# A transformer block in float32 on one core: the second half's gate and up projections as seven products

## The chip, the cores and the metric

The kernel runs on one core of a Trainium2 chip. The metric is the device time of one execution in microseconds (us); of several runs the median is compared. The core has five engines that run side by side, each through its own queue in order: TensorE (PE, matrix products and transposes; its weight loads are listed as PEld), VectorE (DVE), ScalarE (ACT), GpSimd (POOL) and SyncE (SP), whose queue issues the DMA transfers.

## The reference

The input `x` is 2048 rows of 1024 float32. The block is

```
x = x + layernorm(attention(layernorm(x)))        # 16 heads of 64, causal, rotary
x = x + layernorm(ffn(layernorm(x)))
ffn(y): gate = y @ Wg.T;  up = y @ Wu.T           # Wg, Wu: 2752 x 1024
        inter = silu(gate) * up                   # 2048 x 2752
        return inter @ Wd.T                       # Wd: 1024 x 2752
```

`Wg`, `Wu` and `Wd` come as codes from 0 to 15 (int32) with one scale for each block of 64 inputs. A weight is the code's entry in a fixed table of 16 values times the scale.

## The kernel before

The work has four stages: queries, keys, values and attention; the output projection with its layer norms; gate and up; down. All matrices are float32. Gate/up and down take three matmuls for each product (`mm3`, L110): every operand is split into a rounded high part (`A.copy`, on ScalarE, L120) and the rest (a subtraction on VectorE, L121), and high times high, high times rest and rest times high are summed in one PSUM bank of 128 x 512.

**Projection.** For each row tile `t` of 128 rows, `project` multiplies by `Wo`, whose parts lie in the SBUF slots `w`, `xc` and `pa`. `finish_rows` adds the residual, normalizes and stores the normalized rows to DRAM (`yd`). `fill_x2` reads them back and transposes them on TensorE (8 transposes of 128 x 128 for a row tile), and each transposed piece is split into `x2[c]`, the operand of gate/up for the row block `c` of 512 rows. There are four row blocks; all four are held in SBUF.

**Gate and up.** The 2752 outputs are cut into 22 index tiles of 128 (the last is of 64), taken in the order `PAIRS`: 0, 11, 1, 12 and so on. For one index tile `gate_up_weights` looks up 2048 columns of weights (128 gate and 128 up outputs for each of 8 slices of the inputs), 512 at a time, in `looked_up` (L517): codes and scales are loaded, VectorE converts the codes to float (L530), ScalarE makes five straight or bent lines of the code (L535, L537), VectorE combines them by minimum and maximum and multiplies by the scale (L541 to L545), and `split` makes the two parts in `wt`. Then `gate_up` (L599) runs each of the four row blocks against it: 8 slices x 3 matmuls for gate, the same for up, each into a bank of its own (`any_bank` goes round all eight). ScalarE applies Silu to gate out of its bank (L619), VectorE multiplies by up out of the other (L620).

**What down needs.** Down is done already as seven products of half matrices in place of eight (Strassen's method in Winograd's form, `PRODUCTS`). Its left operands A11, A12, A22, S1 to S4 are combined from the results of gate/up on GpSimd (L632 to L640) and stored in DRAM (`aq`). Its right operands come from `down_weights` (L645), two lookups of 512 columns after each index tile; GpSimd combines them (L665 to L674) and they are stored (`bq`). So of each index tile there are four row blocks of matmuls, four lookups for gate/up and two for down.

The order on each engine is set by a scheduler that takes, by priority in the order of the program, what is ready by its own estimate of time; slots of one tag are handed out as they come free. All the transfers in question are issued from SP's queue, in order.

Of the kernel before, what the change touches and what calls it, by code (L numbers as in the profile page):

```python
# [57 lines left out]
def block_kernel(ctx, tc, x, wq, wk, wv, wo, gu_codes, gu_scales, d_codes, d_scales, cos_sin, out):  # L58
# [11 lines left out]
    SLOTS = {"hd": (7, 8), "w": (3, 8), "xc": (4, 8), "pa": (6, 8), "pb": (2, 4), "f4": (4, 4), "pw": (3, 4), "t2": (3, 2), "ol": (1, 2)}  # L70
# [39 lines left out]
    def mm3(o, w, xx, first, last):  # L110

        r = T.matmul(o, lhsT=w[:, 0], rhs=xx[:, 0], start=first, stop=False)  # L112
        T.matmul(o, lhsT=w[:, 0], rhs=xx[:, 1], start=False, stop=False)  # L113
        T.matmul(o, lhsT=w[:, 1], rhs=xx[:, 0], start=False, stop=last)  # L114
        return r
# [53 lines left out]
    at = [dram.tile([E, 512], F32, tag=f"at{c}", name=f"at{c}") for c in range(NC)]  # L169
    x1d = dram.tile([S, E], F32, tag="x1d", name="x1d")  # L170
# [327 lines left out]
    def finish_rows(t, y, beside=False):  # L498
        residual(t, y, slot("f4" if beside else "pb", [P, E], F32, "x1"))
        load(yd[t], y)  # L500
# [16 lines left out]
    def looked_up(codes, s0, s1, rows, tags=None, m=None):  # L517

        if tags:
            c8, sc = (slot(tag, [P, 512], F32, "cs") for tag in tags)  # L520
        else:
            cs = slot("pw", [P, 2, 512], F32, "cs")
            c8, sc = cs[:, 0], cs[:, 1]
# [4 lines left out]
        if m is None:  # L528
            m = slot("f4", [P, 2, 512], F32, "m")[:, 0]
        V.tensor_scalar(c8, c8.bitcast(I32), 1.0, -8.0, ALU.mult, ALU.add)  # L530

        def line(ab):
            ln = slot("t2", [P, 512], F32, "ln")
# [12 lines left out]
        return m  # L546

    def gate_up_weights(n, tags=None):
        it = PAIRS[n]
        w = it_cols(it)  # L550
        wt = [slot(tag, [P, 2, 4, w], FR, "wt") for tag in ("hd", "pa" if n % 2 else "hd")]
        kk = 512 // w

        def columns_of(k0):
            n = kk * w
            off = it * KE * 256 + k0 * w
            t = wt[k0 // 4][:, :, k0 % 4 : k0 % 4 + kk, :]
            m = looked_up(
                gu_codes[:, off : off + n], gu_scales[0:1, off : off + n], gu_scales[1:2, off : off + n], P, tags
            )  # L560
            split(t[:, 0].rearrange("p k n -> p (k n)"), t[:, 1].rearrange("p k n -> p (k n)"), m)
# [116 lines left out]
    for c in range(2):  # L678
        gate_up(*todo[0], c)
# [163 lines left out]
```

## Time and profile before

| | |
|---|---|
| three runs | 3007.55, 3008.38, 3016.82 us; median 3008.38 |
| span of the profiled execution (first to last instruction) | 3001.2 us; its own time outside the span isn't given |
| granted TensorE clock, mean | 0.995 |
| busy over the span: PE, DVE, ACT, POOL | 2908.5, 2032.8, 1701.8, 953.9 us |
| gate/up matmuls (L112 to L114, `bk<-x,wt`) | 3 x 1376, from 1620.9 to 2570.8 us |
| down matmuls (`bk<-bt,at`) | 3 x 616 |
| gate/up from 1725 to 2475 us: PE, DVE, ACT, POOL busy | 750.0, 519.9, 420.0, 160.5 of 750 us |
| 128 x 512 operations: lookup line on ACT, combination on DVE, on POOL | 717 ns; 685 ns or more; 1290 to 1740 ns |
| 128 x 1024 split: ACT, DVE | 1051 and 1279 ns |
| DMA traffic, mean | 179 GB/s |

How it is read: "busy" is the time in which at least one instruction of the engine is open. Instructions of one engine can overlap, so what one of them takes from the engine is the distance from its start to the next start, where the engine waits for nothing, and not its duration. In a group, `out<-in` are the program's tile names, with partitions x elements.

### The profile page before, as it was taken

To read this page: it belongs to the slowest core of one execution; us is meant where nothing else is said; L and a number is where in the kernel's file an instruction comes from. 1 tells how busy PE (TensorE), PEld (TensorE's weight loads), DVE (VectorE), ACT (ScalarE), POOL (GpSimd) and SP (SyncE) were. 2 spreads that over 40 slices of the span, in tenths; PEclk is the share of its full clock that TensorE was granted. 3 is DMA by queue.
4 is the path that set the end of the run, shared out by engine and by line. 5 is a ranking of instruction groups with operands and counts; after the bars stand their busy time and mean duration, and the time that the engine had idled before them with its cause. 6 is when DMAs were issued, how large, how long until landed. Compare 5 with 4: busy or idle time off the path is not lost.

```text
span 3001.2 us, 42583 instructions
## 1 busy us (share of the span) xinstructions
PE 2908.5 (97%) x14192; PEld 2403.6 (80%) x14192; DVE 2032.8 (68%) x4167; ACT 1701.8 (57%) x3573; POOL 953.9 (32%) x1055
## 2 busy tenths in 40 slices
PE   7989999999998999999999999999999999999998
PEld 6868888787877787777788788888888888888887
DVE  5557778787867777777665766776666678444347
ACT  5256767676766666676555655665555566333234
POOL 4344444443444343454322121222211223100034
PEclk9999999999999999999999999999999999999999
DMA  8787665757557558472456444444434444744446
GB/s 290 276 243 232 219 226 170 231 156 234 165 197 195 170 179 254 139 229 92 123 174 219 129 140 135 153 135 137 139 119 136 136 151 153 254 143 143 150 144 235
DMA packets 271740, 536.01 MB, mean 179 GB/s; under 512 B 22944, under 2 KB 113056, under 8 KB 255648
## 3 DMA queue, kind: packets, MB, share of 16 engines
q1 hardware_dynamic: 269344, 529.10, 54.8%
q10 hardware_dynamic: 2176, 4.19, 0.4%
q8 instruction: 112, 1.84, 0.3%
q14 instruction: 108, 0.88, 0.1%
HBM read 371.98 MB, written 161.22 MB: 178 GB/s over the span
## 4 chain that ended last, share of the span: by engine, by line
PE 77%; DMA 10%; DVE 6%; ACT 4%; issue 2%; POOL 1%; SPq 0%; POOLq 0%; ACTq 0%; DVEq 0%
PE bk L112 14%; PE bk L113 14%; PE bk L114 14%; PE pt L323 6%; PE qkv L112 5%; PE qkv L113 5%; PE qkv L114 5%; PE o L328 3%; PE o L327 3%; PE s L281 3%; PE s L283 3%; DMA wf<-in_wq 1%; DMA xc<-xd 1%; DMA q<-qs 1%; DMA vs<-vo 1%
## 5 line engine op out<-in xcount | busy, mean ns | idle before, releaser
L313 POOL TENSOR_SCALAR prob<-prob,rc 128x512 f32<-128x512 f32 (+3 forms) x640 | 404.0, 652 | 439.8 <-DVE rc L308 239.0
L113 PE MATMUL bk<-x,wt 128*128 128x512 f32 x1376 | 535.2, 389 | 0.0
L114 PE MATMUL bk<-x,wt 128*128 128x512 f32 x1376 | 535.0, 389 | 0.0
L112 PE MATMUL bk<-x,wt 128*128 128x512 f32 x1376 | 533.8, 390 | 1.0 <-ACT x L120 0.5
L291 ACT ACTIVATE prob<-s,mxs 128x512 f32<-128x512 f32 (+3 forms) x640 | 402.0, 631 | 148.4 <-DVE mxs L289 90.8
L121 DVE TENSOR_TENSOR pw<-pt,pw 128x512 fp32r<-128x512 f32 (+3 forms) x640 | 378.7, 602 | 120.6 <-ACT pw L120 118.7
L537 ACT ACTIVATE ln<-cs,bias 128x512 f32<-128x512 f32 x520 | 360.0, 717 | 112.4 <-DVE m L544 28.6
L120 ACT CAST pw<-pt 128x512 fp32r<-128x512 f32 (+3 forms) x640 | 323.6, 526 | 168.8 <-PE pt L323 137.8
L323 PE MATMUL pt<-ident,prob 128*128 128x128 f32 x2176 | 344.1, 274 | 7.3 <-DVE pw L121 6.1
L323 PEld LDWEIGHTS pt<-ident,prob 128*128 128x128 f32 x2176 | 266.3, 141 | 62.1 <-issue 7.2
L112 PEld LDWEIGHTS bk<-x,wt 128*128 128x128 f32 x1376 | 258.3, 188 | 55.3 <-ACT wt L120 1.2
L114 PEld LDWEIGHTS bk<-x,wt 128*128 128x128 f32 x1376 | 258.3, 188 | 53.9
L113 PEld LDWEIGHTS bk<-x,wt 128*128 128x128 f32 x1376 | 258.4, 188 | 53.2
L289 DVE TENSOR_REDUCE mxs<-s 128x1 f32<-128x512 f32 x384 | 261.2, 682 | 58.2 <-PE s L283 57.1
L281 PE MATMUL s<-k,q 128*128 128x512 f32 (+3 forms) x640 | 264.0, 414 | 22.9 <-ACT prob L291 18.9
L328 PE MATMUL o<-pw,v 128*128 128x512 f32 (+3 forms) x640 | 246.5, 387 | 9.5 <-DVE pw L121 8.7
L327 PE MATMUL o<-pw,v 128*128 128x512 f32 (+3 forms) x640 | 243.1, 380 | 9.6 <-ACT pw L120 7.2
L112 PE MATMUL qkv<-xc,w 128*128 128x512 f32 x576 | 230.2, 400 | 10.5 <-DMA xc<-xd 5.0
L113 PE MATMUL bk<-bt,at 128*128 128x512 f32 x616 | 239.6, 389 | 0.0
L114 PE MATMUL bk<-bt,at 128*128 128x512 f32 x616 | 238.8, 389 | 0.0
L112 PE MATMUL bk<-bt,at 128*128 128x512 f32 x616 | 238.7, 389 | 0.0
L283 PE MATMUL s<-k,q 128*128 128x512 f32 (+3 forms) x640 | 234.7, 369 | 0.0
(150 smaller groups left out, 5518.2 us busy)
## 6 DMA issues: line engine op xcount, KB each, us to landing
xc<-xd SPq DMA_DIRECT2D x96, 1024.0 KB, 9.2
q<-qs SPq DMA_DIRECT2D x128, 256.0 KB, 7.2
ast<-S SPq DMA_DIRECT2D x44, 512.0 KB, 3.8
cs<-in_gu_scales SPq DMA_DIRECT2D x172, 128.0 KB, 3.3
cs<-in_gu_codes SPq DMA_DIRECT2D x86, 256.0 KB, 3.0
A<-in SPq DMA_DIRECT2D x66, 256.0 KB, 2.1
S<-in SPq DMA_DIRECT2D x66, 256.0 KB, 3.1
ast<-A SPq DMA_DIRECT2D x33, 512.0 KB, 4.4
```

The costliest lines, as they stand in the source:

```text
L112: r = T.matmul(o, lhsT=w[:, 0], rhs=xx[:, 0], start=first, stop=False)
L113: T.matmul(o, lhsT=w[:, 0], rhs=xx[:, 1], start=False, stop=False)
L114: T.matmul(o, lhsT=w[:, 1], rhs=xx[:, 0], start=False, stop=last)
L121: return V.tensor_tensor(lo, src, f32(hi), ALU.subtract)
L281: mm = T.matmul(s, lhsT=q[:, 0, j * P : (j + 1) * P], rhs=k[:, b:e], start=True, stop=False)
L283: T.matmul(s, lhsT=q[:, 1, j * P : (j + 1) * P], rhs=k[:, b:e], start=False, stop=True)
L291: A.activation(prob[i][:, j, : e - b], s, AF.Exp, bias=mx, scale=sign, accum_out=sums[:, j % BATCH, i : i + 1])
L313: G.tensor_scalar(p, p, rc[:, jj % BATCH, i : i + 1], 0.0, ALU.mult, ALU.add)
L323: T.transpose(pt[:, j * P : (j + 1) * P], prob[kb // 4][:, j, kb % 4 * P : (kb % 4 + 1) * P], ident)
L327: T.matmul(o[:, cs], lhsT=v[:, kb, :], rhs=pw[:, 0, cs], start=kb == 0, stop=False)
L328: T.matmul(o[:, cs], lhsT=v[:, kb, :], rhs=pw[:, 1, cs], start=False, stop=kb == nk - 1)
L537: A.activation(ln, c8, AF.Prelu, bias=bias_of[ab], scale=ab[0], alpha=ab[2])
```

## The change

Row blocks 0 and 1 (the first 1024 rows) are worked on as before, for all 22 index tiles, in a first pass. Meanwhile the looked-up weights are combined on GpSimd into seven right operands for each index tile (`keep_weights`) and stored in DRAM (`wqd`). Row blocks 2 and 3 follow in a second pass: rows x inputs and inputs x (gate, up) are each cut in 2 x 2 blocks, and seven products of 4 slices x 3 matmuls take the place of eight (class `Group`). Its left operands (A11, A12, A22 and the sums S1 to S4 of the normalized rows) are combined on GpSimd in `finish_rows`, stored in `yq`, read back and transposed by `fill`; its right operands are read back from `wqd` and split anew (`fetch_w`). Four partial sums share a bank and are copied out between additions. Gate times up for these rows moves from VectorE to GpSimd. The last, half-wide index tile is multiplied out as before.

Lookups for gate and up become 1024 wide; the conversion of codes moves from VectorE to GpSimd. The lookups for down move to the second pass, with slots of their own (`tmp`; 14 KB that a smaller DMA scratch, `dynamic_dma_scratch_size`, sets free). On the host the columns of codes and scales are put in another order.

```diff
     def finish_rows(t, y, beside=False):
...
+        i, l, r = t % 4, y[:, :512], y[:, 512:]
+        if t < 8:
+            load(yd[t], y)
+        elif t < 12:
+            load(yq["A11"][:, i], l)
+            load(yq["A12"][:, i], r)
+        else:
+            load(yq["A22"][:, i], r)
+            a = slot("f4", [P, 2, 512], F32, "ya")
+            for j, name in enumerate(("A11", "A12")):
+                load(a[:, j], yq[name][:, i])
+            s1, s2, s3, s4 = (slot("tmp", [P, 512], F32, "ys") for _ in range(4))
+            G.tensor_tensor(s1, l, r, ALU.add)
...
-        V.tensor_scalar(c8, c8.bitcast(I32), 1.0, -8.0, ALU.mult, ALU.add)
+        G.tensor_scalar(c8, c8.bitcast(I32), 1.0, -8.0, ALU.mult, ALU.add)
...
+    def keep_weights(n, m):
...
+            t1, t2, t3, t4 = (slot("tmp", [P, 512], F32, "wd") for _ in range(4))
+            (b11, b12), (b21, b22) = [[m[:, h, a] for a in range(2)] for h in range(2)]
+            G.tensor_tensor(t1, b12, b11, ALU.subtract)
+            G.tensor_tensor(t3, b22, b12, ALU.subtract)
+            G.tensor_tensor(t2, b22, t1, ALU.subtract)
+            G.tensor_tensor(t4, b21, t2, ALU.subtract)
+            kept = (b11, b21, t2, t1, t3, t4, b22)
+        for i, part in enumerate(kept):
+            load(wqd[n][:, i], part)
+    def gate_up_weights(n):
+        it, wt, w = room_w(n)
+        c = 4 * w
+        m = slot("xc", [P, 2, 2, 512] if w == 256 else [P, 2, 512], F32, "m")
+        for h in range(2):
+            cs = slot("w", [P, 2, c], F32, "cs")
...
+            looked_up(*of_columns(it * KE * 256 + h * c, c), P, mh, cs[:, 0], cs[:, 1], "pw")
...
+            split(*(wt[h][:, i].rearrange(flat) for i in range(2)), mh)
+        keep_weights(n, m)
+        return it, wt, w
...
+    def fill(name, tags, of=any_bank):
+        rows = [slot("pw", [P, 2, 512], F32, "yr") for _ in range(2)]
+        for i in range(2):
+            load(rows[i], yq[name][:, 2 * i : 2 * i + 2])
+        xo[name] = [slot(tag, [P, 2, 2, 512], FR, "x2") for tag in tags]
+        for k in range(4):
+            pt = of()
+            for t in range(4):
+                T.transpose(pt[:, t * P : (t + 1) * P], rows[t // 2][:, t % 2, k * P : (k + 1) * P], ident)
+            d = xo[name][k // 2]
+            split(d[:, 0, k % 2], d[:, 1, k % 2], pt)
+    def fetch_w(n):
+        parts = []
+        for i in (0, 2) if n == NIT - 1 else (0, 2, 4, 6):
+            j = min(2, (3 if n == NIT - 1 else 7) - i)
+            st = slot("pw", [P, 2, 512], F32, "ws")[:, :j]
+            load(st, wqd[n][:, i : i + j])
...
+            split(t[:, 0, :j], t[:, 1, :j], st)
...
     for n in range(NIT):
+        if n == 0:
+            todo.append(gate_up_weights(1))
+        if n == NIT - 1:
+            fill("A12", ("xc", "xc"))
+            fill("S2", ("w", "w"))
+            fill("S1", ("w", "pa"))
+        for c in range(2):
+            gate_up(*todo[n], c)
+        if 0 < n < NIT - 1:
+            todo.append(gate_up_weights(n + 1))
+        if n == NIT - 2:
+            fill("A11", ("xc", "xc"))
...
+    def times(o, name, w, start):
+        for k in range(4):
+            mm3(o, w[:, :, k * P : (k + 1) * P], xo[name][k // 2][:, :, k % 2], start and k == 0, k == 3, True)
+    class Group:
...
+        def one(self):
+            self.y = any_bank()
+            self.inter = room_of(self.kt, self.later, 1)
+            times(self.y, "A11", self.w["B11"], True)
+            A.copy(self.inter[:, 0], self.y)
+        def two(self):
+            x = any_bank()
+            times(x, "A12", self.w["B21"], True)
+            V.tensor_tensor(self.inter[:, 0], self.inter[:, 0], x, ALU.add)
+            A.activation(self.inter[:, 0], self.inter[:, 0], AF.Silu)
+        def six(self):
+            times(self.y, "S2", self.w["T2"], False)
+            self.u2 = slot("tmp", [P, 512], F32, "u2")
+            A.copy(self.u2, self.y)
+        def five(self):
+            self.z = any_bank()
+            times(self.z, "S1", self.w["T1"], True)
+        def seven(self):
+            times(self.y, "S3", self.w["T3"], False)
+            A.copy(self.inter[:, 1], self.y)
+            V.tensor_tensor(self.inter[:, 1], self.inter[:, 1], self.z, ALU.add)
+        def four(self):
+            times(self.y, "A22", self.w["T4"], False)
+            g = slot("tmp", [P, 512], F32, "g2")
+            A.activation(g, self.y, AF.Silu)
+            G.tensor_tensor(self.inter[:, 1], self.inter[:, 1], g, ALU.mult)
+        def three(self):
+            times(self.z, "S4", self.w["B22"], False)
+            V.tensor_tensor(self.u2, self.u2, self.z, ALU.add)
+            G.tensor_tensor(self.inter[:, 0], self.inter[:, 0], self.u2, ALU.mult)
+            for odd in range(2):
+                made(self.kt, self.later, 1, odd)
...
+    for n in range(NIT - 1):
+        now.one()
+        if before:
+            before.four()
+        else:
+            fill("S3", ("hd", "hd"), of_t)
+        now.two()
+        if before:
+            before.three()
+        else:
+            fill("A22", ("hd", "hd"), of_t)
+        ahead = Group(n + 1) if n < NIT - 2 else fetch_w(NIT - 1)
+        now.six()
+        if not before:
+            fill("S4", ("pa", "pa"), of_t)
+        now.five()
+        now.seven()
+        for j in range(2):
+            down_weights(n // 2, 2 * (n % 2) + j)
+        now, before = ahead, now
...
+    last_tile(2, (("A11", now[0]), ("A12", now[1])))
+    before.four()
+    for kt in range(2):
+        ready["A11", kt] = fetch("A11", "B11", kt, True)
+    last_tile(3, (("S1", now[0]), ("A22", now[2])))
+    before.three()
```

`made` holds the combinations and stores that stood at the end of `gate_up` (L632 to L640).

## The prediction

> **What bounds the kernel now.** I read the engine shares on the page first, then the busy time by stretch for the gate/up stage, then TensorE's instructions in order of time, then VectorE and GpSimd side by side.
>
> ```profile
> span 3001.2 us, 42583 instructions
> PE 2908.5 (97%) x14192; PEld 2403.6 (80%) x14192; DVE 2032.8 (68%) x4167; ACT 1701.8 (57%) x3573; POOL 953.9 (32%) x1055
> ```
>
> TensorE is the busiest engine, but an average over stages does not say what the stage to be changed can bear. In the steady part of gate/up:
>
> ```profile
> core 0: us, PE busy (x) PEld busy (x) DVE busy (x) ACT busy (x) POOL busy (x), PEclk, DMA share, GB/s
> 1725.00:2475.00 750.00, 750.00 (x3311) 621.23 (x3310) 519.92 (x762) 420.01 (x656) 160.50 (x104) 1.00 0.42 138
> ```
>
> TensorE never pauses, at the full granted clock (1.00). VectorE is at 69%, ScalarE at 56%. What a matmul costs must not be read from its duration:
>
> ```profile
> 1900.16 0.39 PE L112 MATMUL bk<-x,wt 128*128 128x512 f32 x1
> 1900.39 0.39 PE L113 MATMUL bk<-x,wt 128*128 128x512 f32 x1
> 1900.62 0.39 PE L114 MATMUL bk<-x,wt 128*128 128x512 f32 x1
> ```
>
> One lasts 0.39 us, but the next starts 0.23 us later: they overlap. 750 us / 3311 = 0.2265 us is the price of one. One index tile (192 matmuls) takes 43.5 us of TensorE. The last view is two engines at the same moment, VectorE above and GpSimd below:
>
> ```profile
> 1809.94 0.68 DVE L541 SCALAR_TENSOR_TENSOR mb<-ln 128x512 f32<-128x512 f32 x1
> 1810.54 1.79 DVE L545 TENSOR_TENSOR m<-m,cs 128x512 f32<-128x512 f32 x1
> 1812.25 1.77 DVE L542 SCALAR_TENSOR_TENSOR mb<-ln,mb 128x512 f32<-128x512 f32 x1
> 1814.13 1.60 DVE L543 TENSOR_TENSOR mb<-mb,ln 128x512 f32<-128x512 f32 x1
> 1815.65 0.68 DVE L121 TENSOR_TENSOR wt<-m,wt 128x512 fp32r<-128x512 f32 x1
> ```
>
> ```profile
> 1810.10 1.67 POOL L636 TENSOR_TENSOR in<-in 128x512 f32<-128x512 f32 x1 [17.72 <-DVE in L620]
> 1811.85 1.62 POOL L638 TENSOR_TENSOR in<-in 128x512 f32<-128x512 f32 x1
> 1813.55 1.62 POOL L640 TENSOR_TENSOR in<-in 128x512 f32<-128x512 f32 x1
> ```
>
> While GpSimd combines tiles, VectorE's operations on two SBUF tiles stretch from 0.68 to 1.6 to 1.8 us. Undisturbed they start 0.605 us apart; here three take 1815.65 - 1810.54 = 5.11 us instead of 1.81, so one GpSimd operation takes 1.1 us from VectorE. Operations with one input in PSUM (L620) stayed between 682 and 692 ns in the whole stretch.
>
> **Matmuls removed.** Per index tile the last 1024 rows now need 7 products of 4 x 3 = 12 matmuls, 84, instead of 96. The half-width last tile keeps 48. 21 x 12 = 252 x 0.2265 = 57.1 us less, all on the path, as TensorE never pauses there.
>
> **Transposes added.** Rows 8 to 15 took 8 x 8 = 64, seven operand matrices take 7 x 16 = 112. Eight of them fill 1584.28 to 1585.08 before the next matmul starts, 0.10 us each: 48 x 0.10 = 4.8 us more. TensorE: -52.3 us.
>
> **The first 1024 rows.** Weights for one tile must now come within 96 x 0.2265 = 21.7 us, half of before. VectorE per tile: two halves of five lookup operations and one split, 1024 wide; two 1024-wide splits in the down stage start 1.14 us apart (2643.67, 2644.81), so 12 x 1.14 = 13.7 us. Two multiplications by `u`: 1.2 us. GpSimd: four subtractions for the kept weights and two for the down operands, plus two code conversions 1024 wide (taken from VectorE). No row has such a conversion on GpSimd; L313, one input, lasts 394 ns at 128 columns and 722 at 512, so about 1.0 to 1.2 us at 1024. If VectorE loses 1.1 us to each of the six and 1.0 to each conversion, it needs 13.7 + 1.2 + 6.6 + 2.0 = 23.5 us, more than TensorE. If it loses what it lost on average in the stretch above (by-form groups of L541 to L545 against 685 ns: 64 us over 104 GpSimd operations, 0.61 each), 13.7 + 1.2 + 8 x 0.61 = 19.8 us and TensorE stays the bound. VectorE will be nearly always busy, which is nearer the first row; but GpSimd can slip in beside the two multiplications and in handovers. I take 22.3 us: 20 tiles x 0.6 = +12 us (0 to +36). ScalarE, by its 1242 ns (1024 wide) rows, 10 x 1.24 + 2 x 1.05 + 2 x 0.59 = 15.7 us, fits.
>
> The rule that speaks against this change is in the Trainium skill, "SBUF — State Buffer", section "Who interferes with whom": a VectorE instruction with two SBUF inputs contends with a GpSimd instruction that reads SBUF, and the later one blocks fully. The rows above agree. Taken strictly it would put the sum at its 23.5 us end, where the trace's average put 19.8; I stand between them.
>
> **The last 1024 rows.** TensorE: 84 x 0.2265 = 19.0 us per tile. VectorE: two down lookups 10 x 0.605 = 6.1, splits of the kept weights 3 x 1.14 + 0.6 = 4.0, three additions 1.8: 11.9 us. GpSimd: two multiplications, two combinations of inter, two of down weights (six), and two conversions 512 wide (seven L313 run in 4.17 us, 0.6 each). VectorE with losses: 11.9 + 8 x 0.61 = 16.8 to 11.9 + 6.6 + 1.2 = 19.7 us. ScalarE: 7.2 lines + 3.7 splits + 3 copies and 2 Silu at 0.6 = 13.9 us. TensorE remains just the bound, but one thing is tight. Matrix 7 accumulates into the bank that product 6 left, and must wait until ScalarE has copied it (`u2`); only product 5 lies between, 2.7 us. Likewise matrix 4 waits for `inter[:, 1]`'s copy with one product between. A copy takes 0.6 us and queues behind lookup lines, which wait for VectorE to free `ln`; the longest such waits near here are 0.9 to 1.4 us. Usually it fits. I take 0.5 us per tile: +10 us (0 to +40).
>
> **Moved and hidden.** The kept weights add 7 stores of 256 KB per tile on SP's queue, behind which the next code loads stand. Stores issue in 0.32 us and wait for GpSimd; three staging slots hold the next loads ahead. If that cover went, one landing (3.0 us) per tile would come on top. Traffic per tile: 4.6 MB in 21.7 us, then 4.5 in 19.0: 212 and 237 GB/s, against 256 carried at 2550 to 2625 with TensorE 75.00 of 75. I cost it at nothing. The down lookups leave the first half for the second with their loads and stores, no more in number. The code conversion now queues on GpSimd behind those subtractions, and ScalarE's lines and VectorE wait for it; with the next codes landed ahead it is early, uncovered it costs about 1 us per half tile.
>
> **Start and hand-over.** `Wo` holds `w` and `xc` until the last projection, so tile 1's lookups (load 3 us, conversion, 23 us with the last rows' normalizing between) end some 30 us after it, while tile 0 covers 22: +8 us (0 to +15). The idle 4.0 us in 1640 to 1725 (81.05 of 85) came from waiting for rows 8 to 15, no longer needed there: -4. Between the halves `fill` needs two of three `pw` slots per matrix and a landing of 4 us: +4 (0 to +10).
>
> **Sum.** -52.3 + 12 + 10 + 8 - 4 + 4 = -22 us. The profiled execution has a span of 3001.2 us; its own time is not given, and the median 3008.4 of the runs is 7.2 above the span, time outside it that I leave as it is. 3008.4 - 22 = 2986.
>
> **Rivals.** *TensorE stays the bound throughout* (VectorE loses 0.61 per GpSimd operation, copies always fit): -52.3 + 4 + 4 = 2964. For it: ScalarE and VectorE average 56 and 69% now, and weights are buffered a tile ahead. Against: VectorE's load rises from 519.9 / 17.24 = 30 of 43.5 us per tile to 22.3 + some 18 of 40.7.
>
> *VectorE and GpSimd serialise fully*: 20 x 1.8 + 21 x 0.7 = 51 on -52.3, plus 8: about 3015, no change. For it: the three rows at 1810. Against: GpSimd is idle in most of VectorE's handovers.
>
> *Slower: the copy out of the shared bank.* If VectorE's lag reaches ScalarE's queue in front of `u2` and the `inter[:, 1]` copy, TensorE pauses twice per tile, 42 places. At 1 us each, the size of the ScalarE waits seen, this is 42 us on the forecast: 3028. It decides from (22 + 9) / 42 = 0.75 us per place. For it: before, eight banks rotate and nothing is accumulated onto after a copy. Against: 2.7 us of cover.
>
> **Chances.** TensorE bound 0.25, forecast 0.36 (its own range 2972 to 2999), no change 0.13, slower 0.26. (0.3%, 9 us, is about what a measurement of this kernel can tell from no change.) Faster is 0.25 + 0.36 = 0.61. The range, 2955 to 3032, reaches from the first rival's lower edge to just past the copy's price.
>
> **What would show it.** Right: 3876 gate/up matmuls still 0.2265 us apart; VectorE over 90% in the first half with 1024-wide operations of 1.2 or 2.2 us; TensorE pauses there put to weights (`wt`). Wrong: TensorE at 100% in both halves (first rival), or matmuls waiting for a ScalarE copy of a bank (slower rival), or for a DMA, which I cost at nothing.

## The result and the profile after

The changed kernel takes 3126.13 us (median of four runs, 3124.70 to 3133.40); the kernel before, run beside it, 3012.55. The ratio is 1.0387, 95% interval 1.0363 to 1.041. It is slower by 114 us, where the forecast was 22 us faster and the range ended at 3032. The whole of TensorE's saving arrived, and more than three times as much was lost in pauses and in the slow matmuls after them.

The page of the changed kernel, for the two lines shown of before:

```profile
span 3124.4 us, 42477 instructions
PE 2906.6 (93%) x13988; PEld 2382.7 (76%) x13988; DVE 2198.3 (70%) x3900; ACT 1759.6 (56%) x3478; POOL 1342.3 (43%) x1288
```

TensorE's share falls from 97% to 93%. Its busy time is the same as before with 204 fewer instructions, which already says that some of them ran slower. GpSimd's work grows from 954 to 1342 us. The span is cut at TensorE's first matmul of each part (`wt` for the first 1024 rows, `wr` for the last, `bt` for down), and this table carries the rest of the text:

| | gate/up begins | second pass | down begins | first pass | second pass | down to the end |
|---|---|---|---|---|---|---|
| before | 1620.9 | | 2571.0 | 950.1 together | | 430.2 |
| after | 1630.0 | 2210.1 | 2687.2 | 580.1 | 477.1 | 437.2 |

Of 123.2 us of span, 9.1 lie ahead of gate/up, 107.1 in its two passes and 7.0 in down. (The span lies 11 us below the median of 3012.55 before and 2 us below that of after; hence 123 here and 114 in the medians. Where a run's own time and span are both listed, as 3126.20 and 3124.4, only 1.8 us lie outside the span, so the profiled execution of before was one of its faster ones.) What TensorE needs is 2064 x 0.2265 + 6.4 for 64 transposes = 474 us in the first pass and 1812 x 0.2265 + 4.8 = 415 in the second. So the passes are 106 and 62 us over need. All these are single executions: in the runs below, a pass that an edit doesn't touch took 577.4 to 586.5 us (first) and 474.7 to 477.6 (second), so differences of that size say nothing.

The busy time by stretch, one row for each part, where before had one row with TensorE at 750.00 of 750:

```profile
core 0: us, PE busy (x) PEld busy (x) DVE busy (x) ACT busy (x) POOL busy (x), PEclk, DMA share, GB/s
1630.00:2210.00 580.00, 504.30 (x2131) 409.23 (x2130) 471.18 (x335) 313.28 (x327) 350.53 (x188) 0.93 0.60 199
2210.00:2687.00 477.00, 434.21 (x1862) 348.71 (x1860) 342.16 (x375) 273.42 (x417) 232.12 (x170) 0.98 0.66 218
2687.00:3115.00 428.00, 421.55 (x1848) 347.72 (x1848) 211.95 (x257) 149.43 (x173) 71.57 (x55) 1.00 0.54 181
```

No engine is busy all the time in either pass, and in both the granted clock is under 1.00. TensorE's waits, 1625 to 2209 above the dots and 2210.5 to 2686 below (engine, waiting line, releaser: sum, times, longest):

```profile
PE bk L112 <- ACT wt L120: 41.9, 6, 20.4
PE bk L114 <- DVE wt L121: 29.3, 13, 6.5
...
PE bk L112 <- ACT in L832: 22.5, 15, 3.5
PE bk L112 <- ACT in L813: 15.3, 8, 3.4
```

The passes wait for different things: the first for the two parts of the weights (`split`), the second for ScalarE's copies out of the shared bank. With the `yr` loads and trifles the waits are 76 and 43 us. The other 30 and 19 us are visible only if TensorE is read in order of time:

```profile
1858.45 0.80 PE L112 MATMUL bk<-x,wt 128*128 128x512 f32 x1 [7.00 <-ACT wt L120]
1859.05 0.63 PE L113 MATMUL bk<-x,wt 128*128 128x512 f32 x1
1866.13 0.80 PE L114 MATMUL bk<-x,wt 128*128 128x512 f32 x1 [6.46 <-DVE wt L121]
1866.73 0.63 PE L112 MATMUL bk<-x,wt 128*128 128x512 f32 x1
1867.15 0.63 PE L113 MATMUL bk<-x,wt 128*128 128x512 f32 x1
...
1869.71 0.44 PE L113 MATMUL bk<-x,wt 128*128 128x512 f32 x1
1869.99 0.40 PE L114 MATMUL bk<-x,wt 128*128 128x512 f32 x1
1870.22 0.39 PE L112 MATMUL bk<-x,wt 128*128 128x512 f32 x1
```

After pauses of 7.00 and 6.46 us the matmuls start 0.60, then 0.43 us apart, not 0.23, until 1869.7. The eight from 1866.13 on took 3.6 us instead of 1.8, on top of the pause. Added up over all starts, such slow matmuls cost 23 us in the first pass and 14 in the second. The rest of the 30 and 19 us (7 and 5) lies at the restarts, some 0.2 us each, since a wait is counted from the end of a matmul and the next would have started before it, and in slow transposes. The Trainium skill, "TensorE: Matmul & The Clock Gate", Part 1, says that the clock is halved after an idle window of about 3.4 us and returns after about as long a busy one; this stretch agrees (3.6 us from 1866.13 to 1869.71). Other places show no such sharp bound: after 2.73 us of pause, at 1706.27, seven matmuls were slow, and after 3.32 us, at 2547.16, they were 0.23 us apart from the second on.

VectorE just ahead of the second of these waits, and GpSimd beside it:

```profile
1857.36 2.10 DVE L559 SCALAR_TENSOR_TENSOR m<-ln,m 128x1024 f32<-128x1024 f32 x1
1859.39 2.29 DVE L121 TENSOR_TENSOR wt<-m,wt 128x1024 fp32r<-128x1024 f32 x1
1861.60 2.05 DVE L560 TENSOR_TENSOR m<-m,cs 128x1024 f32<-128x1024 f32 x1
1863.57 0.68 DVE L680 TENSOR_TENSOR in<-bk,in 128x512 f32<-128x512 f32 x1
1864.17 1.90 DVE L121 TENSOR_TENSOR wt<-m,wt 128x1024 fp32r<-128x1024 f32 x1
```

```profile
1856.13 2.25 POOL L594 TENSOR_TENSOR wd<-m,wd 128x512 f32<-128x512 f32 x1
1858.46 2.13 POOL L595 TENSOR_TENSOR wd<-m,wd 128x512 f32<-128x512 f32 x1
1860.67 1.91 POOL L545 TENSOR_SCALAR cs<-cs 128x1024 f32<-128x1024 int32 x1
1863.73 1.26 POOL L592 TENSOR_TENSOR wd<-m 128x512 f32<-128x512 f32 x1 [1.16 <-DVE m L560]
```

VectorE is without a gap, and beside GpSimd its wide operations last 1.9 to 2.3 us instead of the 1.21 of others in the same pass. TensorE starts 0.06 us after the split of 1864.17 ends. Ahead of that split VectorE worked on lookups (L559, L560) of a later tile.

### The profile page after: what moved, and what is told of

Read it like the earlier page. It is cut to its first block, busy times and chain, and to the rows that moved or that the text cites. A ratio compares the mean times of both kernels' runs of the same rounds, so it can differ in the third digit from the quotient of the medians.

```text
span 3124.4 us, 42477 instructions
## 1 busy us (share of the span) xinstructions
PE 2906.6 (93%) x13988; PEld 2382.7 (76%) x13988; DVE 2198.3 (70%) x3900; ACT 1759.6 (56%) x3478; POOL 1342.3 (43%) x1288
## 5 line engine op out<-in xcount | busy, mean ns | idle before, releaser
L121 DVE TENSOR_TENSOR pw<-pt,pw 128x512 fp32r<-128x512 f32 (+3 forms) x640 | 378.8, 602 | 118.8 <-ACT pw L120 117.0
L552 ACT ACTIVATE ln<-cs,bias 128x512 f32<-128x512 f32 (+1 forms) x360 | 319.7, 908 | 247.7 <-POOL cs L545 128.6
L112 PE MATMUL bk<-x,wt 128*128 128x512 f32 x688 | 277.6, 403 | 41.9 <-ACT wt L120 41.9
L114 PE MATMUL bk<-x,wt 128*128 128x512 f32 x688 | 275.6, 402 | 29.4 <-DVE wt L121 29.3
L112 PE MATMUL bk<-x,wr 128*128 128x512 f32 x604 | 240.4, 401 | 39.8 <-ACT in L832 22.5
L113 PE MATMUL bk<-x,wt 128*128 128x512 f32 x688 | 275.3, 400 | 0.0
L113 PE MATMUL bk<-x,wr 128*128 128x512 f32 x604 | 239.3, 396 | 0.0
L114 PE MATMUL bk<-x,wr 128*128 128x512 f32 x604 | 233.2, 395 | 0.9 <-DVE wr L121 0.8
```

The costliest lines, as they stand in the source:

```text
L121: return V.tensor_tensor(lo, src, f32(hi), ALU.subtract)
L552: A.activation(ln, c8, AF.Prelu, bias=bias_of[ab], scale=ab[0], alpha=ab[2])
```

## The experiments: the first pass

**The order of lookups and splits.** Between 1690 and 2090 the groups of the changed kernel, kept apart by shape, show how many halves (1024 columns, half of a tile's weights) VectorE looked up (first combination) and how many it split:

```profile
L556 DVE SCALAR_TENSOR_TENSOR m<-ln 128x1024 f32<-128x1024 f32 x37 | 65.1, 1761 | 0.4
L121 DVE TENSOR_TENSOR wt<-m,wt 128x1024 fp32r<-128x1024 f32 x32 | 61.6, 1926 | 5.7 <-ACT wt L120 5.7
```

37 against 32: lookups run ahead of the splits, from at most 2 halves at the start of the pass to 6 or 7 at 1950 to 2090. The first experiment holds a lookup's first combination behind the split two halves back.

```diff
-        V.scalar_tensor_tensor(m, line(CODES_9_12), CODES_9_12[3], low, ALU.add, ALU.max)
+        ins = V.scalar_tensor_tensor(m, line(CODES_9_12), CODES_9_12[3], low, ALU.add, ALU.max)
+        if behind:                      # splits[-2]
+            after(ins, behind)
```

> One edit to the changed kernel: on VectorE a half tile's lookup may not start before the split of the half tile two before it (before the edit the order let lookups run up to seven halves ahead of the splits). Theory A, order: the first pass lost some 106 us to what TensorE needs for it because VectorE did lookups that could wait, 5 halves of 11 us each, before splits that TensorE waited for; it gets shorter by about 55 us (35 to 75), to 3070. Theory B, rate: VectorE and GpSimd together need 22 to 23.5 us per tile and set the pace whatever the order; 3126, within 10 us.

Measured: 3075.41 us, ratio 1.0204 (1.0144 to 1.0264); the first pass takes 533.8 us, 46 less, the second pass the same 477. Its waits in the first pass, then its stretch of 400 us, and that of the changed kernel:

```profile
PE bk L112 <- ACT wt L120: 21.7, 2, 19.7
PE bk L114 <- DVE wt L121: 14.4, 8, 4.1
```

```profile
1690.00:2090.00 400.00, 385.48 (x1661) 315.68 (x1660) 380.01 (x247) 248.53 (x246) 279.87 (x140) 0.98 0.66 214
```

```profile
1690.00:2090.00 400.00, 350.92 (x1452) 282.67 (x1451) 387.42 (x246) 248.71 (x244) 277.66 (x140) 0.94 0.65 213
```

VectorE does the same number of operations (247 and 246), but 1661 matmuls fit beside them and not 1452. In this run VectorE made 36 splits in the 400 us: 22.2 us for a tile, with VectorE busy for 21.1 of them, where the prediction had 22.3. The amount of VectorE's work was priced nearly rightly; which of it came first was not looked at.

**GpSimd's subtractions for the kept weights.** They are left out with the order as changed, and then with the lookups held back as well:

```diff
-            G.tensor_tensor(t1, b12, b11, ALU.subtract)   # and t3, t2, t4
-            kept = (b11, b21, t2, t1, t3, t4, b22)
+            kept = (b11, b21, b12, b12, b22, b22, b22)
```

> The changed kernel without the four subtractions per tile of the kept weights on GpSimd; as many tiles are stored, with other contents (this leaves out part of the computation). Theory B, rate: VectorE loses 4 x 1.1 us per tile less, 22 becomes 17.6 us, below TensorE's 21.7, and nearly all of the first pass's pauses and slow clock go: about -90 us, 3036. Theory A, order: the lookups still run ahead of the splits, so no more than half of that goes, -20 to -45 us, 3080 to 3106.

> The lookups held two halves ahead of the splits, as in the run with the split first, and the four subtractions of the kept gate and up weights on GpSimd left out (unsubtracted tiles are kept in their place). The two edits alone took 46 and 61 us off the first pass of 580 us, whose matmuls and transposes need 474. Theory 'two parts of one debt' (VectorE is full, and both the order and GpSimd's subtractions matter only while it is behind): together they take 75 to 85 us, the first pass becomes 495 to 505, and what is left is the pause of about 20 us at the start with the clock after it; the whole about 3045. Rival 'two separate costs': 107 us together, so the first pass reaches its 474, the whole about 3018. If the first pass stays at 519 or more, the order costs nothing once GpSimd is quiet.

Measured: 3057.76 us (ratio 1.0145, 1.0085 to 1.0206) and 3056.45 (1.0142, 1.0099 to 1.0186); first passes of 519.2 and 506.8 us. The costs are not separate (46 and 61 alone, 73 together). Without the subtractions VectorE is seldom behind, and the order matters little (12 us, from 519.2 to 506.8). In the run with both edits, 400 us of the first pass are as full as before the change:

```profile
1690.00:2090.00 400.00, 400.00 (x1767) 331.20 (x1766) 351.16 (x275) 266.17 (x271) 130.99 (x77) 1.00 0.72 232
```

Of the 33 us left over 474, 24 lie ahead of 1690: one wait of 20.7 us for the first parts of tile 1, and slow matmuls after it. The other 9 lie in the `fill`s at the end of the pass, 4.7 of them in waits for `yr` loads.

**That pause at the start.** In the changed kernel it ends at 1672.46, since the first wide lookup operation of VectorE starts only at 1659.90. The load of tile 0's looked-up weights (`wb`, 1 MB, landing after 10.1 us) was issued in this stretch, where the DMA share was 0.99 (1625 to 1650). It was moved to a later tile with the subtractions and stores that use it, on top of the held-back lookups.

```diff
-    load(m, wb); keep_weights(0, m)          # ahead of the first pass
+        if n == 1:                           # inside it
+            load(m, wb); keep_weights(0, m)
```

> The kernel with the splits ahead of later lookups, and in it the reading back and combining of the first tile's kept weights (1 MB read, 7 stores, 4 subtractions) moved from the start of the first pass to behind its second tile. Start theory: the pause of 20 us in front of the second tile comes from transfers and GpSimd work of that moment (the transfers' share was 0.99 there); it falls to 8 us or less and the first pass from 534 to about 515, 3075 to 3057. Rival: the pause is set by the last rows' normalizing in front of the lookups; the pause stays at 18 us or more, 3075 within 8.

Measured: 3079.04 us (1.0228, 1.0178 to 1.0278), first pass 533.7. The pause is 16.1 us instead of 19.7, between what the two theories expected, and the pass gains nothing. So that load makes at most 4 us of the pause. The other candidate, normalizing of the last rows that stands ahead of the lookups, was not tried.

**The conversion on GpSimd.** Two runs, one with the change and one without it:

```diff
-        G.tensor_scalar(c8, c8.bitcast(I32), 1.0, -8.0, ALU.mult, ALU.add)     # after
+        V.tensor_scalar(c8, c8.bitcast(I32), 1.0, -8.0, ALU.mult, ALU.add)
```

> The changed kernel with the conversion of codes back on VectorE (one line), for all lookups. Theory F, GpSimd's queue: the waits of ScalarE's lines for the conversion in the second pass go, 119 us to below 50, and the second pass falls by 25 to 45 us; the first pass changes little, as VectorE gains by one lock what it pays in its own time (0.34 us per 512 columns before): about 3090. Theory E, SP's queue: the loads come as late as before and VectorE now waits for them in front of its other work: second pass unchanged or some 10 us longer, 3120 to 3140.

> The kernel before, with the conversion of codes moved to GpSimd and nothing else. With 43.5 us of TensorE work per tile and VectorE at 69%, all theories expect little: within 9 us of before. If it costs 15 us or more by itself, the conversion's place in GpSimd's queue is harmful without the second pass.

Measured: 3122.55 us with the conversions back on VectorE (1.0373, 1.0333 to 1.0413; first pass 573.0, second 482.2), and 3014.91 for the kernel before with its conversions on GpSimd (1.0019, 1.0 to 1.0037). The place of the conversion costs little by itself (4 us in each, which is within the spread of the runs). In the second pass the wait only changes its owner; VectorE now stands where GpSimd stood:

```profile
DVE cs L545 <- DMA cs<-in_d_codes: 88.1, 30, 8.2
```

## The experiments: the second pass

A chain of the changed kernel, in order of time, shows what stands ahead of such a copy (GpSimd, then SyncE's queue, GpSimd, ScalarE, TensorE; rows of other instructions left out):

```profile
2430.28 1.73 POOL L844 TENSOR_TENSOR in<-in,u 128x512 f32<-128x512 f32 x1
2432.04 0.32 SPq L651 DMA_DIRECT2D A<-in  x1
2432.41 0.42 SPq L542 DMA_DIRECT2D cs<-in_d_codes  x1
...
2435.03 0.62 POOL L545 TENSOR_SCALAR cs<-cs 128x512 f32<-128x512 int32 x1 [1.65 <-DMA cs<-in_d_codes]
...
2435.68 1.95 ACT L552 ACTIVATE ln<-cs,bias 128x512 f32<-128x512 f32 x3 [7.07 <-POOL cs L545]
...
2437.53 0.56 ACT L813 COPY in<-bk 128x512 f32<-128x512 f32 x1
...
2438.15 0.50 PE L112 MATMUL bk<-x,wr 128*128 128x512 f32 x1 [2.92 <-ACT in L813]
```

GpSimd's multiplication ends at 2432.01. The store of its result goes 0.03 us later, and the code load, next in SyncE's queue, right behind it. GpSimd waits 1.65 us for the codes, its conversion ends at 2435.65 and ScalarE's three lines start at once, the copy stands behind the lines, and TensorE behind the copy. Every link is the end of a queue that is served in order. The experiments cut the chain at each link.

**Leaving out whole parts.** The lookups of down are left out, or GpSimd's combinations.

```diff
-        looked_up(d_codes[...], ..., m, c8, sc, "t2")                 # first run
+        V.memset(m, 0.0)
-            G.tensor_tensor(first[:, 1], first[:, 1], second[:, 1], ALU.add)   # second run: these
-            G.tensor_tensor(t1, b12, t1, ALU.subtract)                # and the other six, in pass two
```

> The changed kernel without the lookups for down (their loads, conversion, lines and combinations; zeros are combined and stored instead, so this leaves out part of the computation). If the lookups in ScalarE's and SP's queues are what delays the copies, the second pass falls from 477 to about 420 us, 3126 to about 3068. If reading and splitting the kept weights is what delays, it stays above 455 us, 3105 or more.

> The changed kernel with GpSimd's combinations of the second pass left out: the four of the activations' tiles of the second half of the rows and the four of each down tile, the tiles kept uncombined. Theory 'GpSimd paces it' (the code conversion of a down lookup waits on GpSimd behind combinations that wait for loaded tiles, and their slot loads wait behind that on SyncE): the second pass falls from 477 us to 425 to 440, the whole by about 40 us. Rival 'the code loads pace it' (the conversion waits for its codes whatever stands ahead of it): the second pass stays at 460 or more.

Measured: 3058.78 us (1.0148, 1.0119 to 1.0178), second pass 423.0, down 430.3; and 3074.29 (1.0202, 1.0158 to 1.0245), second pass 429.8, down 431.1. The second run's stretch of that pass:

```profile
2213.00:2643.00 430.00, 421.18 (x1862) 345.44 (x1861) 305.38 (x374) 273.62 (x421) 105.02 (x90) 1.00 0.73 246
```

Nearly all of the 44 lookups are still made in it, and conversions still wait for codes, but TensorE waits for only 9 us, runs at a clock of 1.00, and DMA carries more (246 GB/s against 218). So the price needs both: the lookups' chain over four queues, and GpSimd's combinations with the stores that wait for them. The 7 us in down are gone in both runs, but also in four runs below that leave nothing out (430.1 to 431.5), so what they come from stays open.

**More cover.** The product that hides each copy is doubled by another order of the products (four after two, three after five).

```diff
         now.one()
-        if before: before.four()
         now.two()
-        if before: before.three()
+        if before: before.four()
         ...
         now.five()
+        if before: before.three()
         now.seven()
```

> The changed kernel with the products of the second pass in the order 1, 2, 4 of the tile before, 6, 5, 3 of the tile before, 7, so that two products (5.4 us) instead of one (2.7 us) lie between a copy out of the shared bank and the next addition to it. Theory C, cover: TensorE's pauses for the copies of lines 813 and 832 (38 us and some 15 us of slow clock after them) fall by half or more: -20 to -45 us, about 3095. Theory D, the second pass is paced by the chain of loads, conversions and lookups itself: the waits go elsewhere, within 10 us of 3126.

Measured: 3134.33 us (1.0399, 1.0369 to 1.0429), second pass 480.0. The waits at the first copy fall to 5.0 us, those at the last one stay at 23.1, and new ones for the `wr` parts appear. The waits come to 38 us as against 43, with 20 us of slow matmuls as against 14: with more cover the waits mostly moved to other places.

**Copies ahead of the lines.** Each lookup's first bent line is held behind a copy out of the bank.

```diff
+            held_back.append(now.first_copy)          # second lookup of the group before
+            down_weights((n - 1) // 2, 2 * ((n - 1) % 2) + 1)
...
+        held_back.append(now.last_copy)               # first lookup of this group
+        down_weights(n // 2, 2 * (n % 2))
```

> The changed kernel, except that in the second pass over the last 1024 rows the lookup lines of the down matrix stand behind the copies out of the shared bank on ScalarE, not ahead of them: the first lookup of a column group behind the group's last copy, the second behind the first copy of the next group. Theory 'the queue' (TensorE's pauses of the second pass, 38 us put to the two copies and some 15 us of clock after them, come from lookup lines that wait for codes ahead of the copy): the second pass falls from 477 us to 430 to 440, as without the lookups (423) plus the lines' own time, and the whole by about 40 us, to 3086. Rival 'the chain' (the lookups of a group, with their loads and GpSimd's combinations, take as long as the group, so wherever they stand they set the pace): the second pass stays at 465 or more and the down products start with waits for their weights.

Measured: 3129.61 us (1.0385, 1.034 to 1.043), second pass 468.7. Its waits there:

```profile
PE bk L112 <- ACT wr L120: 16.1, 10, 4.1
PE bk L114 <- DVE wr L121: 12.1, 11, 1.9
```

The 38 us of waits for copies are gone, and 28 us of waits for the parts of the read-back weights stand in their place, which ScalarE and VectorE make behind the same lines. The pass is 8 us shorter. The copy was where most of the delay showed, not where it came from.

**Single links.** Three runs cut one each: the code loads of down issued by ScalarE and not by SyncE; GpSimd's last combinations written over tiles whose stores have landed; the code loads issued at the head of the group.

```diff
-            load(c8[r : r + rows].bitcast(I32), codes)         # nc.sync
+            q(c8[r : r + rows].bitcast(I32), codes)            # first run: nc.scalar, down only

-            G.tensor_tensor(m, m, t1, ALU.subtract)            # second run; S4 in the same way
+            G.tensor_tensor(t1, m, t1, ALU.subtract)

     for n in range(NIT - 1):
+        for j in range(2):                                     # third run
+            down_codes_in(n // 2, 2 * (n % 2) + j)
         now.one()
```

> The changed kernel with the code and scale loads of the down lookups issued from ScalarE's queue instead of SP's. Theory E: in the second pass these loads stand in SP's queue behind stores that wait for GpSimd (the load at 2432.4 went 0.4 us after such a store), so the conversion, ScalarE's lines and with them the bank copies come late; then ScalarE's waits for the conversion (119 us) and TensorE's for the copies (38 us) fall to a third and the second pass from 477 to some 430 us: -30 to -50, about 3085. Theory F: the conversion is late because of what stands before it in GpSimd's own queue: the waits stay, within 10 us of 3126. ScalarE may also block on a load whose slot is not free: then slower.

> Nothing left out. In the second pass GpSimd's last combination of each set is written over a tile whose store has long landed, not over the tile whose store was issued just ahead of it (the fourth combination of a down tile over T2; the fourth of the activations over the half that is finished and stored first). In the changed kernel GpSimd stood 39.5 + 36.2 us in these two places between 2215 and 2685, with the next lookup's conversion behind it. Theory 'GpSimd's waits for stores': most of the second pass's 62 us over its need of 415 go, it becomes 435 to 445, the whole about 3090. Rival 'its busy time and its lock' (the combinations themselves are too many): 465 or more, since the number of instructions on GpSimd is the same.

> Nothing left out. The code and scale loads of a group's two down lookups are issued at the head of the group on SyncE, ahead of the stores of the group's combinations, and not one by one when each lookup's turn comes. Theory 'SyncE's queue' (the loads are issued late because stores that wait for GpSimd and VectorE stand ahead of them; ScalarE stood 118.8 us in lines and GpSimd 64.2 us in conversions that waited for codes): the pass falls from 477 to 430 to 445, the whole about 3085. Rival 'GpSimd's queue': the conversion still stands behind combinations, so the pass stays at 460 or more.

Measured: 3118.40 us (1.0359, 1.0303 to 1.0415), second pass 467.5; 3121.92 (1.0366, 1.0321 to 1.041), 475.8; 3129.39 (1.039, 1.0347 to 1.0434), 483 (to the second matmul of down, as the first ran ahead of the pass's end). Ten microseconds, one (within the spread), and none. In the first, ScalarE still waits 108.2 us for conversions. In the third the "early" loads still stand in SyncE's queue behind the stores of the group before.

**Several links at once.** First the held-back lookups with the loads on ScalarE and the lines behind the copies; then the held-back lookups with the two other single edits; then that run with the conversions issued in the middle of the group, ahead of the combinations.

```diff
         now.six()
+        for j in range(2):                                     # third run
+            c8 = down_codes[n // 2, 2 * (n % 2) + j][-2]
+            G.tensor_scalar(c8, c8.bitcast(I32), 1.0, -8.0, ALU.mult, ALU.add)
```

> The changed kernel with three edits that leave nothing out: the lookups held two halves ahead of the splits (46 us off the first pass alone), the code loads of the down lookups issued by ScalarE (10 us off the second pass alone), and the down lookup lines behind the copies on ScalarE. If the place of the lines is the cause of the second pass's pauses: 46 + 40 = 86 us less, about 3040. If it is not: 46 + 10 = 56 us less, about 3070. Neither is under the kernel before, at 3012.

> The lookups held two halves ahead of the splits, the combinations written over tiles that are already stored, and the down codes loaded at the head of the group: nothing left out. If the second pass's debt is made of the two waits: first pass 534, second 425 to 435, the whole 3030 or a little below. If it is GpSimd's amount of work: second pass 460 or more, the whole 3060.

> The run of the three edits together (second pass 485 us), with one thing changed: GpSimd's conversions of a group's two down lookups are issued in the middle of the group, ahead of the combinations of that group's down tiles, where before each stood behind the previous lookup's combination, which waits for that lookup's last operation on VectorE (GpSimd stood 62.3 + 23.0 + 17.7 us in such waits between 2230 and 2600, and ScalarE 92.3 us in lines that waited for conversions). The number of instructions on each engine is the same. Theory 'in series through GpSimd's queue' (conversion, lines, VectorE, combination, next conversion): the pass falls to 430 to 445, the whole to about 3040. Rival 'GpSimd's amount and its lock': the pass stays at 465 or more.

Measured: 3059.95 us (1.0154, 1.0077 to 1.0231), second pass 453.7; 3088.20 (1.0241, 1.0196 to 1.0286), 485.8; 3082.92 (1.0234, 1.0212 to 1.0257), 486.1. The first is the least disturbed second pass that leaves nothing out, 23 us better than the changed kernel's, where its two edits for that pass won 10 and 8 alone; the whole lies between the two expected times (3040 and 3070). The theory that the delay comes from each conversion standing behind the previous lookup's combination falls with the third: moving it changed nothing. In its trace a code load is issued at 2411.79, right behind a store of GpSimd's at 2411.42, and SyncE's queue stands for long (2200 to 2600, SyncE's waits for VectorE's last lookup operation and for a combination):

```profile
SPq L759 <- DVE mb L569: 70.6, 27, 6.5
...
SPq L759 <- POOL mb L765: 15.3, 8, 5.1
```

**The subtractions in the other pass.** The first pass stores the four blocks as they are, the second loads four and makes the other parts on VectorE. In a second version, beside that, ScalarE's lines read the integer codes, and no conversion is left.

```diff
-            kept = (b11, b21, t2, t1, t3, t4, b22)
+            kept = (b11, b21, b12, b22)
...
+            V.tensor_tensor(t[:, 1], b2[:, 0], b1[:, 0], ALU.subtract)   # in fetch_w, and three more
...
-        G.tensor_scalar(c8, c8.bitcast(I32), 1.0, -8.0, ALU.mult, ALU.add)   # second version
+        # line: A.activation(ln, c8.bitcast(I32), ...), bias ab[1] - 8.0 * ab[0]
```

> The same, and the four subtractions of the kept gate and up weights are moved from GpSimd in the first pass to VectorE in the second: the first pass stores the four blocks as they are, the second loads four and not seven and makes the other three and the fourth's difference itself. The first pass should be the 507 us of the run that left them out. The second takes 20 x 4 x 0.68 us = 54 us more of VectorE, which was busy 342 of 477 us there: if it stays under the pace of TensorE the pass keeps the 430 to 460 of the run beside it and the whole is 3000 to 3035; if VectorE becomes the bound beside GpSimd's work the pass goes to 490 and nothing is won.

> The run with the blocks kept as they are (passes of 506 and 502 us), and no conversion on GpSimd at all: ScalarE's lines read the integer codes themselves, the shift by 8 is in the line's constant. Nothing is left out. This takes some 40 wide conversions of the first pass and 44 narrow ones of the second away from GpSimd, and with them the step of the lookup that stands in GpSimd's queue. Theory 'in series through GpSimd's queue': the second pass falls to 430 to 450, the first to 490 to 505, the whole is 2995 to 3025, the level of the kernel before. Rival 'GpSimd's amount and its lock': 20 to 30 us off the second pass at most (34 us of 232 of GpSimd's work go), the whole about 3045. If VectorE, with 412 us of work in that pass, is the bound, the pass stays above 470.

Measured: 3073.67 us (1.0204, 1.0174 to 1.0235), passes of 506.8 and 502.2; 3062.45 (1.0168, 1.0149 to 1.0186), passes of 504.1 and 497.1. The first pass gets the 507 us of the run that left the subtractions out, now with nothing left out. Against the run with the three edits (passes of 537.8 and 485.8) the first version wins 31 us in the first pass and gives 16 back in the second, where taking the conversion away altogether wins 5 us. Of all versions that compute everything, 3060 (the three edits with ScalarE's loads) and 3062 us (the last) are the best. None comes under the kernel before.

## Why the prediction was wrong

**TensorE: right.** The 3876 gate/up matmuls are there (3 x 688 and 3 x 604), 0.2265 us apart where nothing disturbs them. The run without GpSimd's combinations had a second pass of 429.8 us, 15 over the 415 worked out.

**First 1024 rows, +12 (0 to +36): the price nearly right, the step wrong.** 22.3 us for a tile of VectorE was taken, and 22.2 measured, 21.1 of them busy. That it came so near is in part luck: 22.3 was a choice between 19.8 and 23.5. The step that failed compared two totals, VectorE's 22.3 with TensorE's 21.7, as if VectorE did each tile's work when TensorE needed it. VectorE works through its queue in the order that the scheduler wrote down beforehand, with lookups up to 7 halves ahead of splits, so TensorE starved while VectorE worked on what nobody yet needed. From 2125 to 2150, when TensorE still had tiles to do, VectorE was busy for 4.7 of 25 us. Of the 106 us over need, the order took 46, the subtractions with the order mended 27, the start 24 and the `fill`s at the end 9. (Taken the other way round, the subtractions are 61 and the order 12: the two share one cost, and the 27 alone lie inside the range of 0 to 36.)

**Start, +8 (0 to +15): mis-sized.** One pause of 20.4 us, and 26 with the slow matmuls up to 1690. Tile 1's first parts came 43 us after the last projection (1629.4 to 1672.4), where 30 had been taken for the whole tile; tile 0 covered the 22 it was to cover.

**Last 1024 rows, +10 (0 to +40): 62.** The slower rival named copies out of the shared bank, and nearly their price: 37.8 us in 23 waits against 42 at 42 places. Of the two copies it named, that of `inter[:, 1]` (L832) has 22.5 us of the waits and that of `u2` (L824) none; the other 15.3 us went to the copy of the first product (L813), which it had not named. So the near price is luck in part. Its cause was not VectorE's lag in front of ScalarE: ScalarE's lines waited for VectorE in some 20 us of the pass, and 118.8 us for conversions on GpSimd. And the rival counted the copies' pauses alone, without the 19 us of slow matmuls and restarts that follow.

**Moved and hidden, "I cost it at nothing": the step that failed in the second pass.** SyncE's stores wait for GpSimd (some 125 us in the pass) and for VectorE's last lookup operation (75.7 us), and the down codes are loaded behind them only when their turn comes. The three slots that were to hold the next loads ahead (`w`) serve the first pass; the down lookups take their codes into `tmp`. The text put a price on the lost cover, one landing of 3.0 us per tile. Over 21 groups that is 63 us, and the pass is 62 over its need; the numbers agree, but that a landing is what each group loses isn't shown, and loading the codes earlier on SyncE (second pass 483 us) won nothing.

**The clock** was in no term. Slow matmuls added 23 and 14 us to 76 and 43 us of waits, and with restarts and transposes the passes came to 106 and 62 over need.

**Hand-over, +4 (0 to +10): in the range,** some 6 us of waits for `yr` loads, to which slower transposes add about 3 in the first pass. The 9 us ahead of gate/up were in no term; among the kernels run here that start moved between 1624 and 1638, and its cause wasn't tried.

**The signs.** What the prediction named for being right came: 0.2265 us, VectorE over 90% in the steady part (387.4 of 400 us between 1690 and 2090, though 471 of 580 over the whole pass), operations of 1.2 or 2.2 us, pauses put to `wt`. They came together with one for being wrong, the waits for ScalarE's copies; none of them told the size.

**What stays open.** Shown is that the second pass's 62 us need both the down lookups and GpSimd's combinations: without the lookups 8 us are left, without the combinations 15. Not shown is which of the combinations' effects does it: their stores in SyncE's queue, their time in GpSimd's own, or the stretched VectorE operations beside them. Leaving them out removes or lessens all three, and every single link that was cut left the others.

## What to carry to other kernels

Before an engine's load is compared with the time it has, see in what order it serves its consumers: an engine that is just full and works ahead of need can starve its consumer as an overfull one would (46 us here). Where engines pass work on through several in-order queues, follow one item through all of them, stores included, because a load that waits behind a store waits for whoever makes the stored tile. And add to each pause of TensorE that outlasts a few microseconds the slow matmuls that follow it.

## What the runs showed of the hardware

A pause of 6.46 us in TensorE was followed by 3.6 us of matmuls 0.43 us apart; over the first pass of the changed kernel such slow matmuls cost 23 us beside 76 us of pauses, and the granted clock came to 0.93. Pauses of about 3 us had slow matmuls behind them in some places and not in others. A 512-wide GpSimd operation on two SBUF tiles lasted 2.1 to 2.3 us beside VectorE's 1024-wide ones, against 1.26 for one that began beside one with an input in PSUM, while theirs went from 1.21 to as much as 2.3. And ScalarE's lines read int32 codes directly in the last version, in the place of a conversion of 0.6 to 1.9 us on GpSimd.
